# Pauses between gathers, a bias row in bf16 limbs, and a block that advances by two parts

## The chip, the cores and the metric

The kernel runs on one core of a Trainium2 chip. The metric is the device time of one execution, in microseconds (us); before the change it is 374.39 us in the median of three runs (374.32 to 375.45). TensorE (PE) multiplies matrices, VectorE (DVE) and ScalarE (ACT) work elementwise, GpSimd (POOL) here mainly issues indirect DMAs (gathers), and SyncE (SP) issues the plain ones. Each engine works through its own queue in order.

## What is computed

Two graph layers over one graph of N = 2708 nodes with 128 features. The adjacency matrix `adj` is dense in form but has few entries; it holds each node's own loop and is divided by its row sums.

```
# layer 0, hyperbolic
XW   = mobius_matvec(W, X)
sq   = sum(XW * XW, -1);  gamma = 2 / max(1 - sq, EPS)
nominator   = A_hat @ (gamma * XW)
denominator = _clamp_abs(A_hat @ (gamma - 1))
m    = mobius_scalar_mul(0.5, nominator / denominator)
AXW  = mobius_scalar_mul(A_hat.sum(-1), m)
x    = layernorm(x + expmap0(relu(logmap0(AXW))))
# layer 1, message passing
s, d = x @ msg_w[:, :D].T,  x @ msg_w[:, D:].T
messages   = gelu(s[:, None, :] + d[None, :, :] + msg_b)
aggregated = einsum('ijd,ij->id', messages, adj)
h    = gelu(concat([x, aggregated], -1) @ upd_w.T + upd_b) + x
x    = layernorm(x + (layernorm(h) * ln_w + ln_b))
```

The messages exist for all pairs of nodes, but only those with an entry in `adj` count.

## The kernel before, in words

The nodes lie in 22 row blocks of 128. **Layer 0** goes through the blocks one after the other. For each, SP's queue brings a block of the transposed matrix (1408 KB), TensorE multiplies it densely (`mp`, L339), and ScalarE turns it into signs (`sgn`, L334). From the signs TensorE and VectorE make keys (L366) and take from them the list of the block's entries, in tiles of 128 edges, 99 tiles in all. VectorE writes the places of the entries in memory (`F`, L464), and a gather per tile fetches their values from `adj` in DRAM into `V` (99 gathers, L197). The end of layer 0 (`layer0_end`, in three chunks of blocks) forms the first layer norm, the products s and d, and writes d into `table_dram`; the table's first ten blocks are there earlier than the rest.

**Layer 1** works through 26 messages of up to four tiles (512 edges). `fetch` issues the gathers of a message, one per tile, each of 128 rows of 512 bytes from `table_dram` into one of seven rooms `dd`. `messages` then takes one of them: X = R s per tile on TensorE (L687, R the one-hot matrix of receiving rows), the weighted one-hot matrix `rv` per tile on VectorE (L689), dd = X + dd on VectorE (L692), a Gelu over the whole room on ScalarE (L693), and a matmul per tile that adds up the rows of a block (`mp`, L702). After it come a `fetch` for a later message, and a `step`.

A block whose sums are complete becomes a generator, `node`, in `queue`. Its parts are a copy of the sums to SBUF (`agT`, L622), `update` (L566 to L570: two or three f32 matmuls, the bias row as a matmul of one partition, L569, and a Gelu), `first` (adding x, the statistics) and, with the last block of a group, `finish` (L576 to L606): the two layer norms of the group and the output DMA on SP's queue. The groups have 8, 6, 4, 2 and 2 blocks. `step` advances each queued generator by one part. `messages` also calls it when a fourth set of sums would be open.

The first nine messages use only early blocks of the table and the early tiles of the first eight blocks; their gathers are issued during layer 0, from block 14 on, and they themselves run while the last chunk of layer 0 ends. `whole` becomes non-empty when the table is complete; only then are the other messages fetched. The last six messages follow the count of entries that decides whether a dense path, not taken with these inputs, is needed. In the code's order the calls stand in one stream, but a scheduler orders the instructions of each engine by priority, as far as their data allow.

Every gather goes through one helper, `gather` (L195 to L202). After the indirect DMA it puts three writes of one f32 column on POOL's queue (L202), tied to the gather by `issue_after` and given a high priority, so that they follow it on the queue at once; they write to a tile `gap` that nothing reads. `ones`, a 128x128 f32 tile, is written by POOL at the start (L125); it serves the bias row, the count at the end, and `touch`, which calls a function once on ScalarE so that its table is loaded early.

Of the kernel before, what the change touches and what calls it, by code (L numbers as in the profile page):

```python
# [9 lines left out]

F32 = mybir.dt.float32
U32 = mybir.dt.uint32
BF16 = mybir.dt.bfloat16
I32 = mybir.dt.int32
AF = mybir.ActivationFunctionType
OP = mybir.AluOpType
AX = mybir.AxisListType

P = 128
# [16 lines left out]
SPLIT, BITS = 10, 16  # L36
# [42 lines left out]
def hyperbolic_then_message_kernel(  # L79
# [10 lines left out]
    nc = tc.nc  # L90
    N, D = adj.shape[0], P
    assert N % 2 == 0
    NB = (N + P - 1) // P
# [27 lines left out]
    ident = const.tile([P, P], F32, name="ident")  # L121
    make_identity(nc, ident)

    ones = const.tile([P, P], F32, name="ones")
    nc.gpsimd.memset(ones, 1.0)  # L125

    nhalf = const.tile([P, 1], F32, name="nhalf")
    nc.gpsimd.memset(nhalf, -0.5)
    ones_b = const.tile([P, P], BF16, name="ones_b")
    nc.gpsimd.memset(ones_b, 1.0)  # L130
    tri = const.tile([P, P], BF16, name="tri")
# [59 lines left out]
    of_block = {b: [l for l, v in enumerate(LISTS) if v[0] == b] for b in range(NB)}  # L191


    gap = [const.tile([P, 3], F32, name=f"gap{k}") for k in range(2)]

    def gather(o, src, at, kind):
        last = nc.gpsimd.indirect_dma_start(  # L197
            out=o, out_offset=None, in_=src, in_offset=bass.IndirectOffsetOnAxis(ap=at, axis=0)
        )
        with tc.issue_after(last.ins), tc.high_priority():  # L200
            for k in range(3):
                nc.gpsimd.memset(gap[kind][:, k : k + 1], 0.0)  # L202

    mx = big.tile([P, NB, D], F32, name="mx")
    y = big.tile([P, NB, D + 2], F32, name="y")
# [2 lines left out]
    def bank(name, bufs=2):  # L208
        return ps.tile([P, 512], F32, name=name, bufs=bufs)
# [11 lines left out]
    def cols(n):  # L221
        count[0] += 1
        return sc.tile([P, NB], F32, name=f"c{count[0]}")[:, :n]
# [46 lines left out]
    def touch(func, after):  # L270

        nc.scalar.activation(cols(1), after[:, 0:1], func)
# [4 lines left out]
    fin = ctx.enter_context(tc.tile_pool(name="fin", bufs=4))  # L277


    ss_x, ss_m = cols(NB), cols(NB)  # L280
    touch(AF.Ln, ones)
    quads = [(g, min(4, NB - g)) for g in range(0, NB, 4)]
    for g, n in quads:
        mp = bank("kx")
# [188 lines left out]
    def layer0_end(b0, b1):  # L473
# [2 lines left out]
        n = b1 - b0  # L476
        sb = slice(b0, b1)
        count[0] = 0
        touch(AF.Ln, ones)

# [80 lines left out]
    def update(h, k, b, ags):  # L563
        up = bank("sel", 1)
        s = slice(b * P, (b + 1) * P)
        nc.tensor.matmul(up[:, :D], lhsT=x1T[:, s], rhs=wT[:, 2, :], start=True, stop=False)  # L566
        for ag in ags:
            nc.tensor.matmul(up[:, :D], lhsT=ag, rhs=wT[:, 3, :], start=False, stop=False)
        nc.tensor.matmul(up[:, :D], lhsT=ones[0:1, :], rhs=rowvec["ub"][0:1, :], start=False, stop=True)  # L569
        nc.scalar.activation(h[:, k, :], up[:, :D], AF.Gelu)  # L570

    def finish(h, b0, n, pool, last):
# [57 lines left out]

    queue = []

    def step():

        for g in list(queue):
            if next(g, queue) is queue:
                queue.remove(g)

# [31 lines left out]
    def fetch():  # L670

        if len(rooms) < (len(work) if whole else ahead):
            dd = edge.tile([P, 4, P], F32, name="dd", bufs=RING)
            for k, (_, t, *_) in enumerate(work[len(rooms)]):
                gather(dd[:, k, :], table[: SPLIT * P] if t in soon else table, J[:, t : t + 1], 1)
            rooms.append(dd)

    def messages():

        q, ts = done[0], work[done[0]]  # L680
        done[0] += 1
        w = len(ts)
        dd = rooms[q][:, :w, :]
        X = bank("kx" if q >= ahead and q % 2 else "X").rearrange("p (t d) -> p t d", d=D)[:, :w, :]
        rv = edge.tile([P, 4, P], F32, name="rv", bufs=2)
        for k, (b, t, *_) in enumerate(ts):
            nc.tensor.matmul(X[:, k, :], lhsT=R[:, t, :], rhs=s_nm[:, b, :], start=True, stop=True)  # L687

            nc.vector.tensor_scalar(  # L689
                rv[:, k, :], iotaN, rid[:, t : t + 1], V[:, t : t + 1], op0=OP.is_equal, op1=OP.mult  # L690
            )
        nc.vector.tensor_tensor(dd, X, dd, op=OP.add)  # L692
        nc.scalar.activation(dd, dd, AF.Gelu)  # L693
        for k, (b, t, first, final, before) in enumerate(ts):
            mine = before or b >= EARLY
            if first:
                while len(sums) > 2:
                    step()
                sums[b] = bank("mp", 3)
                if mine:  # L700
                    own(b, sums[b])
            nc.tensor.matmul(  # L702
                sums[b][:, :P], lhsT=dd[:, k, :], rhs=rv[:, k, :], start=(first and not mine), stop=final
            )
            if final and before:
                nc.scalar.copy(gd[:, b, :D], sums.pop(b)[:, :P])
            elif final:
                g0, gn = group[b]
                queue.append(node(gd[:, g0 : g0 + gn, :D], b - g0, b, g0, gn, [gd[:, b, :D]] if b < EARLY else []))
        fetch()  # L710
        step()


    ends, found, placed = [], [], []
# [91 lines left out]
    cnt = sc.tile([P, 2], F32, name="cnt")  # L806
    nc.vector.tensor_reduce(cnt[:, 0:1], signs, axis=AX.X, op=OP.add)
    nc.vector.tensor_reduce(cnt[:, 1:2], deg.rearrange("p l k -> p (l k)"), axis=AX.X, op=OP.add)
    bp = bank("sel", 1)
    nc.tensor.matmul(bp[:, 0:2], lhsT=ones, rhs=flags, start=True, stop=True)  # L810
    nc.tensor.matmul(bp[:, 2:4], lhsT=ones, rhs=cnt, start=True, stop=True)
# [115 lines left out]
```

## Time and profile before

| what | before |
|---|---|
| median of 3 runs | 374.39 us (374.32 to 375.45) |
| profiled execution: its time, its span | 370.8 us, 369.1 us |
| mean granted clock of TensorE | 0.886 |
| busy: PE, PEld, DVE | 295.7, 272.9, 276.9 us |
| busy: ACT, POOL | 199.5, 239.0 us |
| start of the first gather after layer 0 | 257.64 us |
| end of the last gather | about 340.3 us |
| last dd add, end of VectorE's last instruction | 344.06, 364.37 us |

The profiled execution is one of its own, somewhat shorter than the median; 1.7 us of it lie outside the span. A line of the page's fifth part, or of an answer for one line, reads: line of the kernel, engine, operation, output and inputs, count | busy us in all, mean ns of one | idle us of the engine just before it, and what ended most of this idle time. A line of a table of windows gives the stretch, its length, the busy time of each engine with its count of instructions, TensorE's granted clock as a share of full speed, the share of DMA and its GB/s. A line of a timeline gives the start, the duration, the engine, the line, the operation, and in brackets the idle time ahead of it.

### The profile page before, as it was taken

To read this page: it belongs to the slowest core of one execution; us is meant where nothing else is said; L and a number is where in the kernel's file an instruction comes from. 1 tells how busy PE (TensorE), PEld (TensorE's weight loads), DVE (VectorE), ACT (ScalarE), POOL (GpSimd) and SP (SyncE) were. 2 spreads that over 40 slices of the span, in tenths; PEclk is the share of its full clock that TensorE was granted. 3 is DMA by queue.
4 is the path that set the end of the run, shared out by engine and by line. 5 is a ranking of instruction groups with operands and counts; after the bars stand their busy time and mean duration, and the time that the engine had idled before them with its cause. 6 is when DMAs were issued, how large, how long until landed. Compare 5 with 4: busy or idle time off the path is not lost.

```text
span 369.1 us, 8354 instructions
## 1 busy us (share of the span) xinstructions
PE 295.7 (80%) x2427; PEld 272.9 (74%) x2427; DVE 276.9 (75%) x1544; ACT 199.5 (54%) x537; POOL 239.0 (65%) x889
## 2 busy tenths in 40 slices
PE   2618998999999999999998897409858997996700
PEld 3507998999999898999998797409747886995600
DVE  0998898978768796877787878983725586477994
ACT  2791476767756885987659394424411232225340
POOL 7500087988898717078889878940888888888000
PEclk9955999999999999999999998957985699599755
DMA  8900455244564472556675210100122122122211
GB/s 305 386 2 2 168 173 196 102 166 163 205 227 179 160 241 105 183 191 214 205 265 203 96 50 1 31 14 28 48 54 56 51 52 52 52 56 50 63 59 38
DMA packets 16016, 45.16 MB, mean 122 GB/s; under 512 B 5402, under 2 KB 10926, under 8 KB 13150
## 3 DMA queue, kind: packets, MB, share of 16 engines
q1 hardware_dynamic: 9486, 37.43, 27.8%
q0 software_dynamic: 6336, 6.55, 7.4%
q10 hardware_dynamic: 144, 0.60, 0.5%
q8 instruction: 20, 0.33, 0.3%
q14 instruction: 30, 0.25, 0.2%
HBM read 41.74 MB, written 2.83 MB: 121 GB/s over the span
## 4 chain that ended last, share of the span: by engine, by line
PE 52%; DVE 13%; DMA 11%; POOL 11%; ACT 9%; issue 3%; POOLq 0%; DVEq 0%; ACTq 0%; SPq 0%
PE mp L339 22%; POOL dd L197 9%; DMA aT<-in_adj_t_dram 8%; PE kx L366 6%; PE sel L454 5%; PE mp L702 4%; ACT sgn L334 3%; PE X L540 3%; PE X L687 3%; DMA dd<-table_dram,J 2%; PE kx L287 2%; POOL gap L202 2%; ACT junk L294 2%; DMA xT<-in_x_t_dram 1%; PE kx L360 1%
## 5 line engine op out<-in xcount | busy, mean ns | idle before, releaser
L197 POOL DMA_INDIRECT V<-in_adj_dram,F x99 | 95.8, 968 | 69.1 <-DVE F L464 44.8
L339 PE MATMUL mp<-y,aT 128*128 128x130 f32 x968 | 126.8, 283 | 1.6 <-DMA aT<-in_adj_t_dram 1.6
L339 PEld LDWEIGHTS mp<-y,aT 128*128 128x128 f32 x968 | 117.3, 194 | 2.0 <-DMA aT<-in_adj_t_dram 2.0
L197 POOL DMA_INDIRECT dd<-table_dram,J x99 | 96.2, 971 | 27.4 <-PE X L687 13.4
L334 ACT ACTIVATE sgn<-aT 128x2816 bf16<-128x2816 f32 x22 | 56.0, 2547 | 7.3 <-DMA aT<-in_adj_t_dram 7.2
L702 PE MATMUL mp<-rv,dd 128*128 128x128 f32 x198 | 33.2, 320 | 14.0 <-ACT dd L693 12.3
L366 PEld LDWEIGHTS <-sgn 128*128 128x128 bf16 x484 | 28.6, 100 | 17.2 <-issue 9.0
L702 PEld LDWEIGHTS mp<-rv,dd 128*128 128x128 f32 x198 | 29.4, 226 | 15.9 <-ACT dd L693 13.9
L366 PE MATMUL kx<-kd,sgn 128*128 128x128 bf16 x484 | 33.3, 223 | 7.5 <-ACT sgn L334 7.5
L202 POOL MEMSET gap<- 128x1 f32 x594 | 36.3, 123 | 0.1
L689 DVE TENSOR_SCALAR rv<-iotaN,rid,V 128x128 f32<-128x128 f32 x99 | 30.9, 359 | 4.0 <-PE mp L702 4.0
L693 ACT ACTIVATE dd<-dd 128x512 f32<-128x512 f32 (+2 forms) x26 | 15.7, 607 | 30.6 <-DVE dd L692 30.6
L454 PE MATMUL sel<-z,R 128*128 128x41 f32 (+5 forms) x198 | 29.0, 277 | 3.6 <-DVE R L430 2.3
L454 PEld LDWEIGHTS sel<-z,R 128*128 128x128 f32 x198 | 25.8, 192 | 6.1 <-DVE R L430 3.7
L425 ACT ACTIVATE work<-iota,mid 128x256 f32<-128x256 f32 (+3 forms) x54 | 28.2, 569 | 3.5 <-DVE mid L418 3.3
L374 DVE MAX8 top<-kx 128x8 f32<-128x128 f32 (+3 forms) x133 | 24.8, 226 | 2.9 <-PE kx L366 2.7
L687 PE MATMUL X<-mx,R 128*128 128x128 f32 x132 | 22.3, 305 | 0.5 <-DVE dd L692 0.5
L687 PEld LDWEIGHTS X<-mx,R 128*128 128x128 f32 x132 | 18.6, 209 | 1.9 <-DVE dd L692 0.6
L692 DVE TENSOR_TENSOR dd<-X,dd 128x512 f32<-128x512 f32 (+1 forms) x17 | 11.3, 670 | 10.7 <-DMA dd<-table_dram,J 10.3
L457 DVE TENSOR_TENSOR work<-sel,place 128x120 f32<-128x120 f32 (+11 forms) x29 | 11.2, 387 | 9.6 <-PE sel L454 9.1
L378 ACT ACTIVATE junk_s<-kx 128x384 bf16<-128x384 f32 (+2 forms) x25 | 12.1, 483 | 9.6 <-DVE top L374 7.8
L622 ACT COPY agT<-mp 128x128 f32<-128x128 f32 x22 | 5.8, 262 | 18.6 <-PE mp L702 15.5
(200 smaller groups left out, 578.8 us busy)
## 6 DMA issues: line engine op xcount, KB each, us to landing
aT<-in_adj_t_dram SPq DMA_DIRECT2D x22, 1408.0 KB, 6.4
V<-in_adj_dram,F POOLq DMA_INDIRECT x99
dd<-table_dram,J POOLq DMA_INDIRECT x99
xT<-in_x_t_dram SPq DMA_DIRECT2D x2, 704.0 KB, 5.5
x_sb<-in_x_nm_dram SPq DMA_DIRECT2D x2, 704.0 KB, 9.3
table_dram<-dt SPq DMA_DIRECT2D x5, 256.0 KB, 2.5
out_dram<-nom SPq DMA_DIRECT2D x4, 256.0 KB, 3.2
pk<-in_pack_dram ACTq DMA_DIRECT2D x1, 587.5 KB
```

The source lines that it names most:

```text
L197: last = nc.gpsimd.indirect_dma_start(out=o, out_offset=None, in_=src, in_offset=bass.IndirectOffsetOnAxis(ap=at, axis=0))
L202: nc.gpsimd.memset(gap[kind][:, k : k + 1], 0.0)
L334: nc.scalar.activation(sgn, aT, AF.Sign, accum_out=signs[:, b : b + 1])
L339: p = nc.tensor.matmul(op[:, : D + 2], lhsT=aT[:, j, :], rhs=y[:, j, :], start=(j == 0), stop=(j == NB - 1))
L366: nc.tensor.matmul(kp[:, i * P : (i + 1) * P], lhsT=sgn[:, j, :], rhs=kd[:, q, :], start=False, stop=(i == len(groups) - 1 and j == j1 - 1),)
L374: nc.vector.max(top[:, c : c + 8], seg[:, s, :])
L425: nc.scalar.activation(r0, iota[:, k0 * P : k1 * P], AF.Abs, scale=2.0, bias=mid[:, k : k + 1])
L454: nc.tensor.matmul(sp[:, k, :], lhsT=R[:, t0 + k0 + k, :], rhs=z, start=True, stop=True)
L687: nc.tensor.matmul(X[:, k, :], lhsT=R[:, t, :], rhs=s_nm[:, b, :], start=True, stop=True)
L689: nc.vector.tensor_scalar(rv[:, k, :], iotaN, rid[:, t : t + 1], V[:, t : t + 1], op0=OP.is_equal, op1=OP.mult)
L693: nc.scalar.activation(dd, dd, AF.Gelu)
L702: nc.tensor.matmul(sums[b][:, :P], lhsT=dd[:, k, :], rhs=rv[:, k, :], start=(first and not mine), stop=final)
```

## The change

It has three parts.

First, the pause. `gap` becomes a tile of 360 bytes per partition, written in one instruction. It follows each gather of V (kind 0) and those table gathers that are issued before `whole` is set (kind 1); table gathers after that have kind 2 and no pause. In the built order 133 gathers have a pause, 99 of V and 34 of the table, and the last 65 of the table have none.

Second, the bias row. At the start VectorE splits it into three bf16 values that sum to it, in three rows of a tile `ub3`. Line L569 becomes one matmul of three bf16 rows of ones with these three rows. `ones` in f32 is no longer made at the start, but by VectorE in a work tile ahead of the count at the end; `touch` for the logarithm uses `iotaN`. A tile `nhalf`, which nothing used, is gone.

Third, the steps. `step` takes a number of generators, all by default; after each message's `step()` a `step(1)` advances the oldest queued block by one more part.

```diff
-    ones = const.tile([P, P], F32, name="ones")
-    nc.gpsimd.memset(ones, 1.0)
-
-    nhalf = const.tile([P, 1], F32, name="nhalf")
-    nc.gpsimd.memset(nhalf, -0.5)
...
-    gap = [const.tile([P, 3], F32, name=f"gap{k}") for k in range(2)]
+    gap = [const.tile([P, 360], U8, name=f"gap{k}") for k in range(2)]
...
-        with tc.issue_after(last.ins), tc.high_priority():
-            for k in range(3):
-                nc.gpsimd.memset(gap[kind][:, k : k + 1], 0.0)
+        if kind < 2:
+            with tc.issue_after(last.ins), tc.high_priority():
+                nc.gpsimd.memset(gap[kind], 0.0)
...
+    ub3 = const.tile([3, D], BF16, name="ub3")
+    limb = small.tile([P, 4 * P], BF16, name="junk_s", bufs=1)[0:3, :D]
+    rest_ub, hold = (small.tile([P, 4 * P], F32, name="work", bufs=3)[0:3, :D] for _ in range(2))
+    nc.vector.tensor_copy(rest_ub, rowvec["ub"][0:3, :])
+    for i in range(3):
+        nc.vector.tensor_copy(limb, rest_ub)
+        if i == 0:
+            nc.vector.tensor_scalar(hold, limb, ident[0:3, 0:1], None, op0=OP.mult)
+        else:
+            nc.vector.scalar_tensor_tensor(hold, limb, ident[0:3, i : i + 1], hold, op0=OP.mult, op1=OP.add)
+        if i < 2:
+            nc.vector.tensor_tensor(rest_ub, rest_ub, limb, op=OP.subtract)
+    nc.vector.tensor_copy(ub3, hold)
...
-    touch(AF.Ln, ones)
+    touch(AF.Ln, iotaN)
...
-        nc.tensor.matmul(up[:, :D], lhsT=ones[0:1, :], rhs=rowvec["ub"][0:1, :], start=False, stop=True)
+        nc.tensor.matmul(up[:, :D], lhsT=ones_b[0:3, :], rhs=ub3, start=False, stop=True)
...
-    def step():
-
-        for g in list(queue):
+    def step(n=NB):
+
+        for g in queue[:n]:
...
-                gather(dd[:, k, :], table[: SPLIT * P] if t in soon else table, J[:, t : t + 1], 1)
+                gather(dd[:, k, :], table[: SPLIT * P] if t in soon else table, J[:, t : t + 1], 1 + len(whole))
...
         fetch()
         step()
+        step(1)
...
+    ones = small.tile([P, 4 * P], F32, name="work", bufs=3)[:, :P]
+    nc.vector.memset(ones, 1.0)
     bp = bank("sel", 1)
     nc.tensor.matmul(bp[:, 0:2], lhsT=ones, rhs=flags, start=True, stop=True)
```

More of the change, by code (lines that the diff above doesn't have):

```diff
@@ L12 @@
 U32 = mybir.dt.uint32
+U8 = mybir.dt.uint8
 BF16 = mybir.dt.bfloat16
@@ L478, in layer0_end @@
         count[0] = 0
-        touch(AF.Ln, ones)
+        touch(AF.Ln, iotaN)
         den, r = nom[:, sb, D], nom[:, sb, D + 1]
```

## The prediction

> **What bounds the kernel now.** I read the page first, for its groups of instructions, and then the chain of waits from 255 us on, because the change has one part that acts only there.
>
> ```profile
> span 369.1 us, 8354 instructions
> PE 295.7 (80%) x2427; PEld 272.9 (74%) x2427; DVE 276.9 (75%) x1544; ACT 199.5 (54%) x537; POOL 239.0 (65%) x889
> ...
> L197 POOL DMA_INDIRECT V<-in_adj_dram,F x99 | 95.8, 968 | 69.1 <-DVE F L464 44.8
> ...
> L197 POOL DMA_INDIRECT dd<-table_dram,J x99 | 96.2, 971 | 27.4 <-PE X L687 13.4
> ...
> L202 POOL MEMSET gap<- 128x1 f32 x594 | 36.3, 123 | 0.1
> ```
>
> The averages say TensorE, and for layer 0 that is so: the windows give PE 94.67 us of the 97 between 43 and 140. POOL has 65%, but in the V row it waits 44.8 us for layer 0's lists (F), in few long stretches: 9.7 us ahead of 137, 11.4 ahead of 158, 13.3 ahead of 257.6. In layer 1 it is otherwise. The windows from the start of layer 1 (columns: length, then PE, PEld, DVE, ACT, POOL busy, TensorE's clock) and POOL's timeline inside one of them:
>
> ```profile
> 275.00:290.00 15.00, 13.04 (x52) 11.63 (x53) 7.42 (x26) 3.35 (x10) 13.18 (x49) 0.50 0.22 55
> 290.00:308.00 18.00, 18.00 (x131) 16.21 (x130) 14.03 (x54) 5.67 (x17) 15.95 (x57) 0.95 0.20 52
> 308.00:327.00 19.00, 16.77 (x94) 15.30 (x92) 10.87 (x50) 4.49 (x13) 16.76 (x61) 0.73 0.21 52
> ```
>
> ```profile
> 279.16 0.94 POOL L197 DMA_INDIRECT dd<-table_dram,J  x1 [0.15 <-issue]
> 280.09 0.18 POOL L202 MEMSET gap<- 128x1 f32 x3
> 280.42 0.94 POOL L197 DMA_INDIRECT dd<-table_dram,J  x1 [0.15 <-issue]
> 281.37 0.17 POOL L202 MEMSET gap<- 128x1 f32 x3
> ```
>
> One gather every 1.266 us: 0.944 for itself, 0.17 for three writes, 0.15 in which POOL waits for nothing that shows. The first gather after layer 0 starts at 257.64, the last ends at about 340.3: 65 gathers in 82.7 us, 1.272 each. The chain from 255 us to the end gives the gathers 29.0%, the pause 5.2% and "issue" 7.1%; VectorE's dd add waits for landing rows 7 times, 17.3 us, as the waits show:
>
> ```profile
> DVE dd L692 <- DMA dd<-table_dram,J: 17.3, 7, 4.2
> ```
>
> So layer 1 goes at the gathers' pace; then, from the last dd add (344.06) to VectorE's last instruction (364.37), 20.3 us of VectorE's chain (two layer norms); then the output DMA, to 369.1.
>
> **What the Trainium skill says.** "Perfetto Trace Analysis", section "DMA Instruction — SWDGE (GPSIMD)": the recorded end is when the last DSP has written its descriptors, and there is no start marker. So the 0.944 us may leave out part of a gather's work. This trace agrees: after an idle POOL, a gather's record starts 0.27 to 0.31 us after the write of F it waited for (45.80 to 46.11, 74.53 to 74.81). "SBUF — State Buffer", section "Who interferes with whom": the port pair shared by VectorE and GpSimd is an exclusive lock, which tensor_scalar can hold or wait for in its two-port mode. The trace shows little of it: the rv write (L689) takes about 405 ns instead of 334 if it starts about 0.5 to 0.65 us into a gather, else the same inside and outside of one. "VectorE: DVE Perf Modes", "Zero memsets can be issued as uint32": one cycle per element whatever the type. That is of VectorE, but POOL's rows agree: 128 elements take 201 ns in f32, 194 in bf16.
>
> **Part 1a, no pause in layer 1 (65 gathers).** In 185 of 198 cases the distance from a gather's end to the next start is 321 to 323 ns, also where the third write lasted until 472: it is not the writes' ends that count. The writes start 28 ns apart, 3 x 28 = 84 ns; the rest, 0.237, is about the lead seen after idle (0.27 to 0.31, some of it the semaphore's). I take it that the lead belongs to the gather and stays: 0.944 + 0.237 = 1.18 a gather. Bounds: 0.945 if the lead overlaps the gather before, 1.266 if it grows to what the pause was. Value: 64 x 0.086 = -5.5 us. Cover: TensorE. From 290 to 308 it is 18.00 of 18.00 busy, and can keep the new pace only because part 2 takes work out of it.
>
> **Part 1b, one write of 360 bytes in layer 0 (133 gathers).** The trace has no such write. From 128x1 (94 ns) to 128x128 (201) a write grows 0.84 ns per element; 360 byte elements occupy 28 + 302 = 0.33 us, the gap is 0.33 + 0.237 = 0.57, the period 1.51. If the bytes go four at a time, 90 elements: 0.10, gap 0.34, period 1.29. I take 1.51. It is hidden in the three idle stretches, 34.3 us together, so long as POOL has caught up by 257.6. Replaying the recorded gathers with their ready times: at a gap of 0.53 the last one is out of the way at 256.8, at 0.57 at 259.3 (1.6 late), at 0.65 at 264.6 (7.0 late), at 0.70 at 269.7 (12.1). In the changed order of the queue, in which V and table gathers mix differently, the same sum at 1.51 ends at 256.2. Between 0 and +1.6: I take +0.8. The first consumers (dd adds at 225.4 to 264.5) have slack: the gather that came at 210.7 would come at 227.6, still before its use.
>
> **Part 2, bias row.** Twice a 1x128 f32 pass for each of 22 updates:
>
> ```profile
> L569 PE MATMUL sel<-pk,ones x44: 270/372/578, 278.5 to 349.6; 1*128 1x128 f32 x44
> ```
>
> The pair advances the chain by 0.41 to 0.43 us (0.72 at half clock); one bf16 pass I estimate at 0.08, from the weight load of the bf16 row L366 (100 ns) with its matmul beside it. So -0.35 x 22 = -7 us of TensorE, nearly all beside gathers. On the end path lie one or two updates: -0.5 (0 to -1). The limbs cost some 11 VectorE operations on three rows at the start, in the waits of two root chains. But in the built order ScalarE loads one activation table more (nine, not eight) as its logarithm now touches iotaN, ready later: 1.283 us a load, on a path that runs through ScalarE from 13.5 to 25.7, of which 0.82 was idle. I take +0.5 (0 to +1.3). The ones that a late VectorE write makes again costs 0.2 us beside waits: nothing, or 0.2 were VectorE the bound there.
>
> **Part 3, two parts for the oldest block.** More instructions of finished blocks stand before each message's successor, fewer after the last. In the built order 119 VectorE instructions are left after the last dd add instead of about 144. By their durations (0.15 to 0.34 us) the 25 are worth 3.1 us, and 20.3 becomes 17.2. They must now fit before: VectorE has 63.2 us busy of the 86 between 257 and 343, so 66 of about 81, and that holds; but the last adds will be held up somewhat by norms ahead of them in VectorE's queue. Other queues: a block's update can now follow its copy (L622, 262 ns on ScalarE) within one message, with the next X matmuls queued behind on TensorE, who feed the next dd add; in the built order other matmuls mostly stand between. The norm's last part issues an output DMA on SP's queue, where by then nothing else is; POOL's queue isn't passed. For all of this +0.7 (0 to +2). With part 2: -3.1 - 0.5 + 0.7 = -2.9.
>
> **Sum**, against the profiled execution: -5.5 + 0.8 + 0.5 - 2.9 = -7.1 on a span of 369.1, so 362.0, and with the 1.7 us around it 363.7 instead of 370.8. The median of the runs is 374.39; the same difference gives 367.3.
>
> **Rivals.** *A, the lead overlaps.* POOL's queue is about two gathers ahead, which speaks for it; that the lead is there after a queued write too speaks against. At 0.98 us, 65 gathers would save 18.6, but TensorE has 72.5 us busy from 257 to 343 and keeps at least 65.5 without the bias passes, with half clock in places: 12 us at most, so 374.4 - 12 + 0.8 + 0.5 - 2.9 = 360.8. *B, the pause is not what sets the pace* (the lead grows, or TensorE, full from 290 to 308, takes its place): only the end's gain is left, 374.4 - 2.9 + 1.3 = 372.8; with a third of the pace 371. *C, slower: pauses in layer 0 that POOL cannot catch up.* The place is the stretch from 158 us to the first gather of layer 1. It decides from a gap of about 0.67 on: there layer 1 starts 8.5 us late and eats the gains. At 0.70 it is 12.1 - 8.0 = +4.1, so 378.5. For it: a byte write may cost more than the f32 slope says, and no row shows one longer than 1x1. Against: bf16 costs no more than f32. The same sign would come of a VectorE held up by unbroken gathers; the flat durations of L689 speak against it.
>
> **Chances.** Forecast 0.50 (364 to 370), A 0.20 (358 to 363), B 0.16 (370.5 to 374), C and its like 0.14 (375 to 382). A measurement of this kernel tells about 0.3% from no change, 373.3 to 375.5. The range reaches into A and to the upper edge of B, 359.5 to 373.5; beyond it I leave some 0.2. Faster 0.80, same 0.06 (B's edge), slower 0.14.
>
> **What will show it.** POOL's timeline after 258: starts 1.18 apart means the lead stays, 0.95 to 1.0 is A, 1.25 is B. In layer 0, a gap of 0.57 or 0.34, and the first gather of layer 1 at 257.6 plus the start's 0.5, or later, which is C. L569 with 22 passes. From the last dd add to VectorE's end 17 us. If the period falls and the end doesn't, the wait at dd L692 will have moved from DMA to TensorE. I am wrong if layer 1 starts more than 3 us late, or VectorE's rv rows grow beyond 0.45 us.

## The result, and the profile after

The changed kernel is slower: 376.68 us in the median of 20 runs (373.86 to 379.0) against 372.55 in 20 runs of the kernel before beside them (369.65 to 375.6). The ratio is 1.0124, with a 95% interval of 1.0097 to 1.0151, so about 4.6 us more. The profiled execution took 378.13 us, in a span of 376.3; that of before took 370.8. Runs of one kernel spread over some 5 us here, and one profile is one draw from that: differences of 2 or 3 us between two traces say nothing by themselves, and times are compared below by their ratios.

The page after, with the rows that answer to those of before (the gathers now stand at L194, the pause at L199, rv at L701):

```profile
span 376.3 us, 7851 instructions
PE 290.7 (77%) x2405; PEld 266.5 (71%) x2405; DVE 289.3 (77%) x1555; ACT 200.8 (53%) x538; POOL 259.2 (69%) x426
...
L194 POOL DMA_INDIRECT V<-in_adj_dram,F x99 | 95.3, 963 | 55.4 <-DVE F L476 39.5
...
L194 POOL DMA_INDIRECT dd<-table_dram,J x99 | 96.1, 971 | 29.0 <-issue 20.0
...
L199 POOL MEMSET gap<- 128x360 uint8 x133 | 56.9, 428 | 0.1
...
L701 DVE TENSOR_SCALAR rv<-iotaN,rid,V 128x128 f32<-128x128 f32 x99 | 33.9, 399 | 4.6 <-PE mp L714 3.4
```

The gathers cost what they did. The 133 pauses cost more than the 594 short writes, 56.9 us instead of 36.3. In front of the dd gathers "issue" has grown from 11.8 to 20.0 us: with no pause behind them, they wait for nothing that shows. VectorE is busy for 12 us more, and its rv row has a mean of 399 ns instead of 359. Before, that row was:

```profile
L689 DVE TENSOR_SCALAR rv<-iotaN,rid,V 128x128 f32<-128x128 f32 x99 | 30.9, 359 | 4.0 <-PE mp L702 4.0
```

POOL's timeline in layer 1 shows where the first part of the gain went (start, duration, and in brackets the idle time ahead):

```profile
282.66 0.95 POOL L194 DMA_INDIRECT dd<-table_dram,J  x1 [0.31 <-issue]
283.92 0.95 POOL L194 DMA_INDIRECT dd<-table_dram,J  x1 [0.30 <-issue]
285.17 0.95 POOL L194 DMA_INDIRECT dd<-table_dram,J  x1 [0.30 <-issue]
286.42 0.95 POOL L194 DMA_INDIRECT dd<-table_dram,J  x1 [0.30 <-issue]
```

A gather starts every 1.25 us, with 0.30 of unexplained idle time between two, where with the pause it was 1.27. The three short writes had cost 0.02 us, not 0.086: they lay in time that POOL spends anyway. The ten traces from chips of this pace agree: from the first gather of layer 1 to the last dd add it is 84.9 to 85.3 us in the six that have no pause there, and 86.2 to 86.9 in the four that have one.

And VectorE and POOL in layer 0, about 248 us, from two answers of the timeline of the same kernel:

```profile
247.94 0.95 POOL L194 DMA_INDIRECT V<-in_adj_dram,F  x1 [0.16 <-issue]
248.88 0.46 POOL L199 MEMSET gap<- 128x360 uint8 x1
249.50 0.95 POOL L194 DMA_INDIRECT V<-in_adj_dram,F  x1 [0.16 <-issue]
```

```profile
247.91 0.22 DVE L260 SCALAR_TENSOR_TENSOR c<-c,c 128x4 f32<-128x4 f32 x1
248.05 0.89 DVE L701 TENSOR_SCALAR rv<-iotaN,rid,V 128x128 f32<-128x128 f32 x1
248.31 0.63 DVE L260 SCALAR_TENSOR_TENSOR c<-c,c 128x4 f32<-128x4 f32 x1
248.38 0.63 DVE L701 TENSOR_SCALAR rv<-iotaN,rid,V 128x128 f32<-128x128 f32 x1
249.00 0.16 DVE L260 SCALAR_TENSOR_TENSOR c<-c,c 128x4 f32<-128x4 f32 x1
```

An rv write that takes 0.34 us alone starts at 248.05, 0.11 us into a gather, and lasts until 248.94: to 0.05 after the gather's end at 248.89. The small instruction behind it waits with it. I call this a hold. For comparison two rv writes of the kernel before, beside a gather that has three short writes behind it:

```profile
234.33 1.02 POOL L197 DMA_INDIRECT dd<-table_dram,J  x1
```

```profile
234.52 0.33 DVE L689 TENSOR_SCALAR rv<-iotaN,rid,V 128x128 f32<-128x128 f32 x1
234.86 0.54 DVE L689 TENSOR_SCALAR rv<-iotaN,rid,V 128x128 f32<-128x128 f32 x1
```

The one that starts 0.19 us into the gather takes its usual 0.33; the one that starts 0.53 into it lasts until just after the gather's end.

By stretches, from the two traces (blocks are counted from 0): block 2's signs, which the expectations below call block 1's, come at 46.0 us instead of 44.5, block 14's at 159.2 instead of 154.6, the last write of the table at 265.7 instead of 254.4, the first gather of layer 1 at 268.90 instead of 257.64. From there to the last dd add it is 85.1 us instead of 86.4, and from that add to VectorE's end 17.7 instead of 20.3. So layer 0 lost some 11 us in these two executions, layer 1 gained 1.3 and the end 2.6.

### The profile page after: what moved, and what is told of

Its sections match the earlier page's. It is cut to its first block, busy times and chain, and to the rows that moved or that the text cites. A ratio compares the mean times of both kernels' runs of the same rounds, so it can differ in the third digit from the quotient of the medians.

```text
span 376.3 us, 7851 instructions
## 1 busy us (share of the span) xinstructions
PE 290.7 (77%) x2405; PEld 266.5 (71%) x2405; DVE 289.3 (77%) x1555; ACT 200.8 (53%) x538; POOL 259.2 (69%) x426
## 5 line engine op out<-in xcount | busy, mean ns | idle before, releaser
L194 POOL DMA_INDIRECT V<-in_adj_dram,F x99 | 95.3, 963 | 55.4 <-DVE F L476 39.5
L351 PE MATMUL mp<-y,aT 128*128 128x130 f32 x968 | 129.0, 286 | 4.3 <-DMA aT<-in_adj_t_dram 4.3
L351 PEld LDWEIGHTS mp<-y,aT 128*128 128x128 f32 x968 | 119.0, 196 | 6.0 <-DMA aT<-in_adj_t_dram 4.6
L194 POOL DMA_INDIRECT dd<-table_dram,J x99 | 96.1, 971 | 29.0 <-issue 20.0
L199 POOL MEMSET gap<- 128x360 uint8 x133 | 56.9, 428 | 0.1
L714 PE MATMUL mp<-rv,dd 128*128 128x128 f32 x198 | 33.1, 317 | 18.8 <-ACT dd L705 17.2
L714 PEld LDWEIGHTS mp<-rv,dd 128*128 128x128 f32 x198 | 28.3, 218 | 21.4 <-ACT dd L705 19.2
L701 DVE TENSOR_SCALAR rv<-iotaN,rid,V 128x128 f32<-128x128 f32 x99 | 33.9, 399 | 4.6 <-PE mp L714 3.4
L466 PE MATMUL sel<-z,R 128*128 128x41 f32 (+5 forms) x198 | 29.7, 279 | 4.5 <-DVE R L442 4.0
L704 DVE TENSOR_TENSOR dd<-X,dd 128x512 f32<-128x512 f32 (+1 forms) x17 | 11.3, 671 | 12.8 <-DMA dd<-table_dram,J 7.1
L699 PE MATMUL X<-mx,R 128*128 128x128 f32 x132 | 20.6, 293 | 0.5 <-DVE dd L704 0.5
L699 PEld LDWEIGHTS X<-mx,R 128*128 128x128 f32 x132 | 17.6, 201 | 1.1 <-DVE dd L704 0.6
L442 DVE TENSOR_SCALAR R<-work,deg 128x512 f32<-128x512 f32 (+3 forms) x32 | 17.4, 557 | 0.8 <-ACT work L437 0.4
```

The costliest lines, as they stand in the source:

```text
L194: last = nc.gpsimd.indirect_dma_start(out=o, out_offset=None, in_=src, in_offset=bass.IndirectOffsetOnAxis(ap=at, axis=0))
L199: nc.gpsimd.memset(gap[kind], 0.0)
L351: p = nc.tensor.matmul(op[:, : D + 2], lhsT=aT[:, j, :], rhs=y[:, j, :], start=(j == 0), stop=(j == NB - 1))
L466: nc.tensor.matmul(sp[:, k, :], lhsT=R[:, t0 + k0 + k, :], rhs=z, start=True, stop=True)
L701: nc.vector.tensor_scalar(rv[:, k, :], iotaN, rid[:, t : t + 1], V[:, t : t + 1], op0=OP.is_equal, op1=OP.mult)
L714: nc.tensor.matmul(sums[b][:, :P], lhsT=dd[:, k, :], rhs=rv[:, k, :], start=(first and not mine), stop=final)
```

## Experiments: which part, and why

Two theories for layer 0 were put against each other, and a third beside them. **L (hold)**: the long write keeps VectorE's two-port instructions waiting. **Q (queue)**: the pause's length alone makes POOL late. **B**: the limbs at the start and the moved steps cost it (this is not the prediction's rival B). A first set took the change apart.

**Three columns again in layer 0**, all else as in the changed kernel:

```diff
-    gap = [const.tile([P, 360], U8, name=f"gap{k}") for k in range(2)]
+    gap = [const.tile([P, 3], F32, name=f"gap{k}") for k in range(2)]
...
-                nc.gpsimd.memset(gap[kind], 0.0)
+                for k in range(3):
+                    nc.gpsimd.memset(gap[kind][:, k : k + 1], 0.0)
```

> The changed kernel with the old pause in layer 0 (three f32 columns after each of the 133 paused gathers, in place of 360 bytes); the rest of the change stays. Theory L (lock): the write of 360 bytes keeps VectorE's two-port instructions waiting until the gather has ended, and layer 0 grows by that; then VectorE's rv rows before 257 us fall back from some 0.5 us to 0.36 on the mean, the last table write comes at 255 to 256 us and not at 265.7, and the time is 0.990 to 0.996 of before (pace of layer 1 -1.3 us, end -2.9, start +1). Theory Q (queue): POOL's longer period alone makes the gathers late; the same time here, but VectorE's rows stay as long as they are now. Theory B (start and order): the loss comes from the limbs at the start and the moved steps; then it stays at 1.01 of before.

Measured: 0.9904 of before (0.9867 to 0.9941), 369.76 us. B falls: with limbs and steps in place the kernel is faster than before. Setting the two ratios against each other (1.0124 / 0.9904), the 360 bytes cost 2.2%, some 8 us. The rv rows of VectorE between 20 and 257 us, first of the changed kernel, then of this one:

```profile
L701 DVE TENSOR_SCALAR rv<-iotaN,rid,V 128x128 f32<-128x128 f32 x24 | 11.0, 538 | 1.5 <-DMA V<-in_adj_dram,F 1.1 <-PE mp L714 0.4
```

```profile
L702 DVE TENSOR_SCALAR rv<-iotaN,rid,V 128x128 f32<-128x128 f32 x24 | 8.0, 355 | 0.0
```

The mean falls from 538 to 355 ns; in the kernel before it is 372:

```profile
L689 DVE TENSOR_SCALAR rv<-iotaN,rid,V 128x128 f32<-128x128 f32 x24 | 8.5, 372 | 0.0
```

So the hold goes with the 360 bytes, as L says; Q had these rows stay as long as they were. The last table write came at 258.9, later than I expected, but 6.8 us before that of the changed kernel.

**360 bytes in the kernel before**, up to the end of layer 0, with three columns afterwards, bias and steps untouched:

```diff
-    gap = [const.tile([P, 3], F32, name=f"gap{k}") for k in range(2)]
+    gap = [const.tile([P, 360], U8, name=f"gap{k}") for k in range(2)]
+    gap3 = const.tile([P, 3], F32, name="gapt")
...
-            for k in range(3):
-                nc.gpsimd.memset(gap[kind][:, k : k + 1], 0.0)
+            if kind < 2:
+                nc.gpsimd.memset(gap[kind], 0.0)
+            else:
+                for k in range(3):
+                    nc.gpsimd.memset(gap3[:, k : k + 1], 0.0)
...
-                gather(dd[:, k, :], table[: SPLIT * P] if t in soon else table, J[:, t : t + 1], 1)
+                gather(dd[:, k, :], table[: SPLIT * P] if t in soon else table, J[:, t : t + 1], 1 + len(whole))
```

> The kernel before with one change: 360 bytes in place of three columns after the gathers that are issued while the table is incomplete; the later ones keep the three columns, bias and steps are as before. L: VectorE's busy time before 257 us grows by 10 us or more, the last table write comes 7 to 10 us later than 254.4, time 1.02 to 1.03 of before. Q: VectorE's rows unchanged, the table write at 254 to 256, only the first gather of layer 1 is late, time 1.01. B: 1.00.

Measured: 1.0121 (1.0057 to 1.0185). The one edit makes the kernel slower by itself, by less than L's 1.02 to 1.03. The sum of VectorE's durations from 20 to 257 us grows by 19 us (instructions that stand together count twice in it: as busy time it is 195.3 us instead of 191.9), and the last table write comes at 263.4, where Q expected 254 to 256. The profile is that of the slowest of the six runs, 382.15 us against a median of 378.12, so its times support those of the changed kernel's trace and prove nothing alone.

**No pause in layer 1**, in the kernel before:

```diff
-        with tc.issue_after(last.ins), tc.high_priority():
-            for k in range(3):
-                nc.gpsimd.memset(gap[kind][:, k : k + 1], 0.0)
+        if kind < 2:
+            with tc.issue_after(last.ins), tc.high_priority():
+                for k in range(3):
+                    nc.gpsimd.memset(gap[kind][:, k : k + 1], 0.0)
...
-                gather(dd[:, k, :], table[: SPLIT * P] if t in soon else table, J[:, t : t + 1], 1)
+                gather(dd[:, k, :], table[: SPLIT * P] if t in soon else table, J[:, t : t + 1], 1 + len(whole))
```

> The kernel before with one change: no pause after the last 65 table gathers. All theories: a start every 1.25 us instead of 1.27, so 64 x 0.02 = 1.3 us less at most, ratio 0.9955 to 1.0. If VectorE's rv rows in layer 1 get longer than 0.36 us without the pause, unbroken gathers hold VectorE up, and the ratio is above 1.

Measured: 0.9939 (0.9908 to 0.9969). The gathers stand 1.25 us apart; from the first gather of layer 1 to the last dd add it is 85.1 us instead of 86.4. The interval's upper end, -1.2 us, fits this; the ratio is a little better. The rv rows after 257 us take 359 ns, so unbroken gathers do not hold VectorE more.

**The bias row alone**, in the kernel before (the limbs, one bf16 matmul at the bias row, `touch` on iotaN; the diff is that of the change without pauses and steps).

> The kernel before with the bias row as three bf16 limbs alone, with all that goes with it (the limbs at the start, touch on iotaN). L and Q: start 0.3 to 1.2 us later (one table load more on ScalarE, limb operations held up to 3 us on VectorE), TensorE relieved by 22 x 0.35, end -0.5: ratio 0.997 to 1.003. B: 1.005 or more, with block 1's signs (44.5 us before) 1.5 us later.

Measured: 0.9998 (0.9966 to 1.0031). Block 2's signs came 2.3 us later, at 46.8, and VectorE's chain at the end took 19.9 us instead of 20.3.

**The second step alone**, in the kernel before:

```diff
-    def step():
-
-        for g in list(queue):
+    def step(n=NB):
+
+        for g in queue[:n]:
...
         fetch()
         step()
+        step(1)
```

> The kernel before with one change: the oldest queued block moves by one more part after each message. From the last dd add to VectorE's end 17.7 us instead of 20.3, as in the changed kernel, layer 0 untouched: 0.991 to 0.996 of before. If the moved parts hold up the messages, the last dd add is later by more than 2 us and the ratio is near 1.

Measured: 0.9979 (0.9957 to 1.0001), so -0.8 us, where I expected more. From the last dd add to VectorE's end it is 20.55 us, no less than before, although only 120 of its instructions start after that add, where before it was 141. The waits of VectorE after 344 us say why:

```profile
DVE nom L616 <- ACT nom L570: 3.0, 2, 2.0
```

It waits 3.0 us for the last blocks' Gelu, which hangs on their updates on TensorE; before, this wait was 0.4. In the five traces from chips of this pace that have both the step and the one-pass bias row, the chain takes 17.67 to 17.83 us, and this wait is 0.2 to 0.4; in the five that lack one or both it takes 19.9 to 22.8. So the fewer instructions pay off only with the shorter update: parts 2 and 3 work together, each alone gives little. For each part alone this is one trace, and is no more than that.

Then the pause's length was parted from the hold.

**Twelve short writes**, about as long a pause in pieces:

```diff
-    gap = [const.tile([P, 360], U8, name=f"gap{k}") for k in range(2)]
+    gap = [const.tile([P, 12], F32, name=f"gap{k}") for k in range(2)]
...
-                nc.gpsimd.memset(gap[kind], 0.0)
+                for k in range(12):
+                    nc.gpsimd.memset(gap[kind][:, k : k + 1], 0.0)
```

> The changed kernel with twelve writes of one f32 column in place of the one of 360 bytes: by 28 ns a write the gap is 0.237 + 12 x 0.028 = 0.57 us, the same pause as the bytes give (0.578), in twelve short pieces. It parts length from hold. Theory L (the long write itself holds VectorE's two-port instructions): period 1.52 as now, but VectorE's rv rows before 257 us back at 0.36 to 0.42 us on the mean, the last table write at 257 to 261, the time 0.985 to 1.0 of before. Theory Q (the longer period makes the gathers late, and late V values and rows do the harm): as slow as the changed kernel, 1.01 to 1.02, with the rv rows at 0.36.

Measured: 1.0115 (1.0063 to 1.0167), as slow as the changed kernel. The gap is 0.577 us in most cases, as worked out, but 30 of the 132 gaps before layer 1 are longer, mostly about 0.77, so that their mean is 0.619, against 0.591 in the changed kernel. And the hold is gone:

```profile
L702 DVE TENSOR_SCALAR rv<-iotaN,rid,V 128x128 f32<-128x128 f32 x24 | 8.2, 367 | 1.8 <-DMA V<-in_adj_dram,F 1.0 <-PE mp L715 0.8
```

The mean is 367 ns, as before the change (372), and the last table write comes at 258.6. So L falls in the form in which I stated it: a pause of about this length makes the kernel as slow without the hold. That it would cost exactly as much at exactly the same length is not shown: over the 65 gathers after 158 us the longer mean is worth some 1.6 us, by my estimate from the two means there, 0.617 and 0.592. The trace shows gathers that are late. POOL from 257 us on:

```profile
258.78 0.95 POOL L194 DMA_INDIRECT dd<-table_dram,J  x1 [0.15 <-issue]
259.73 0.42 POOL L200 MEMSET gap<- 128x1 f32 x12
260.50 0.95 POOL L194 DMA_INDIRECT V<-in_adj_dram,F  x1 [0.34 <-DVE dd L705]
261.44 0.42 POOL L200 MEMSET gap<- 128x1 f32 x12
262.02 0.95 POOL L194 DMA_INDIRECT V<-in_adj_dram,F  x1 [0.15 <-issue]
262.97 0.57 POOL L200 MEMSET gap<- 128x1 f32 x12
263.90 0.95 POOL L194 DMA_INDIRECT dd<-table_dram,J  x1 [0.35 <-issue]
```

POOL comes straight from paused gathers into layer 1, whose first gather is that at 263.90: 5.3 us after the last table write, where before it was 3.2, after 13 us of idle POOL. A gather for V runs as late as 262.02; before the last was at 243.27. The lateness that one sees is 2 us, though, not 8. This profile is the quickest of its kernel's seven runs (373.3 against a median of 376.1) and the profile with three columns the slowest of its ten (371.8 against 369.8), which takes away most of the distance between them; where the rest of the usual loss lies is not seen.

**90 words in place of 360 bytes:**

```diff
-    gap = [const.tile([P, 360], U8, name=f"gap{k}") for k in range(2)]
+    gap = [const.tile([P, 90], F32, name=f"gap{k}") for k in range(2)]
```

> The changed kernel with one write of 90 f32 elements, the same 360 bytes in a quarter of the elements. By 0.84 ns an element the gap falls to about 0.34 us. Q: period as before, so no lateness, 0.990 of before. L: VectorE is held only as long as one write is short: if holding starts with the write's place in the queue and lasts to the gather's end, rv rows stay at about 0.5 us, the time near 1.005; if its length counts, rv rows 0.36 to 0.40 and 0.990 to 0.995.

Measured: 0.9938 (0.9912 to 0.9963). The same bytes in a quarter of the elements give a gap of 0.353 us, no loss, and rv rows without the hold:

```profile
L701 DVE TENSOR_SCALAR rv<-iotaN,rid,V 128x128 f32<-128x128 f32 x24 | 8.3, 365 | 0.8 <-PE mp L714 0.8
```

So it is the number of elements that sets how long the write takes, and neither the bytes nor that it is one write does the harm. Whether a long write of f32 elements would hold VectorE as the 360 byte elements do was not tried: length and type changed together.

**No pause at all:**

```diff
-        if kind < 2:
+        if kind < 0:
```

> The changed kernel with no pause anywhere. Gathers 1.25 us apart where they are queued, in layer 0 too. L and Q: no write is left to hold VectorE, no lateness; rv rows 0.36, time 0.985 to 0.995 of before. If unbroken gathers by themselves hold VectorE more than gathers with three short writes do, rv rows in layer 0 exceed 0.40 us and the time 1.0.

Measured: 0.9897 (0.9837 to 0.9956). The pauses can go in layer 0 too: rv rows have 350 ns there. This version, the one with three columns and the one with 90 words are quicker than both kernels, and their intervals overlap.

**The runs that decide less.** Ten runs were to place the loss further. All of them landed on three other chips, on which the kernel before too took about 500 us, and their traces show long idle times on all engines: from 20 us on, VectorE stands still for more than 1.5 us at a time for some 163 us in all with late limbs, where it is 33 us in the trace of before. What these engines wait for there, the traces don't show. The edits, in the changed kernel: nine or sixteen columns (as twelve above), the long write up to the 69th gather of V and three columns after it, or the reverse:

```diff
+    gap3 = [const.tile([P, 3], F32, name=f"gapc{k}") for k in range(2)]
+    values = [0]
...
+        early = kind == 0 and values[0] < 69
+        values[0] += kind == 0
...
-                nc.gpsimd.memset(gap[kind], 0.0)
+                if early:
+                    nc.gpsimd.memset(gap[kind], 0.0)
+                else:
+                    for k in range(3):
+                        nc.gpsimd.memset(gap3[kind][:, k : k + 1], 0.0)
```

and, on three columns, the limbs made later, by the same instructions put into a function:

```diff
-    touch(AF.Ln, iotaN)
+    touch(AF.Ln, ones_b)
...
+            if b == 14:
+                limbs()
```

> The changed kernel with nine writes of one f32 column as the pause of layer 0: gap 0.237 + 9 x 0.028 = 0.49 us, period 1.44, no long write. The replay of the recorded gathers has POOL just caught up at a gap of 0.50. Theory Q (only the length of the pause counts, through gathers that come late at the start of layer 1): no lateness, 0.990 to 0.995 of before, as with three columns. If the length harms in proportion from the start (late V values and rows hold up VectorE in layer 0): some two thirds of the way from three columns (0.990) to twelve (1.0115), so 1.004. L (the long write's hold): 0.990.

> The changed kernel with its 360 bytes only after the first 69 gathers of V (up to about 158 us, where POOL has idle time to catch up), and three columns after the other 64 paused gathers. L: VectorE's two-port rows are held there; block 14's signs at 158 to 159 us as in the changed kernel instead of 156 with three columns, layer 0 about 3 us longer, time 0.998 to 1.002 of before. Q: POOL catches up before 158, so no cost: 0.990.

> The changed kernel with three columns after the first 69 gathers of V and its 360 bytes after the other 64 paused gathers (158 us to the start of layer 1). Q: the whole loss, 1.010 to 1.013 of before. L: the larger part of it, since VectorE is the busier in that stretch, about 1.003 to 1.008. With the run before, the two losses should add up to that of the changed kernel if the causes are separate.

> The kernel with three columns in layer 0 (0.990 of before), with the limbs made at block 14 instead of at the start, and touch on a tile of ones in bf16 that is ready early. L and Q alike: no ninth table load, first signs as before (44.5 us in block 1 and not 46), so 1 to 1.5 us less than with the limbs at the start: 0.985 to 0.990. If the start's delay is hidden by the wait for the matrix, 0.990.

> As the run of this edit before (three columns after the first 69 gathers of V, 360 bytes after the other 64 paused gathers), on another chip. Theory Q (gathers late at the start of layer 1): the whole loss, 1.010 to 1.013 of before. L (hold by the long write): about 1.003 to 1.008, with rv rows before 257 us at 0.5 us.

> As the run of this edit before (360 bytes only after the first 69 gathers of V, three columns after the other 64), on another chip. Q: 0.990, since POOL catches up before 158 us. L: 0.996 to 1.002, block 14's signs at 158 to 159 us and not 156.

> As the run of this edit before (nine short writes, gap 0.49 us), on another chip. Q: just no lateness, 0.990 to 0.995. Harm in proportion to length: 1.004. L: 0.990.

> As the run of this edit before (three columns in layer 0, limbs made at block 14, touch on bf16 ones), on another chip. 0.985 to 0.990 if the start's delay counts, 0.990 if it is hidden. By the table that the trace then shows, signs of block 1 at 44.5 us.

> The changed kernel with its 360 bytes only after the first 69 gathers of V, three columns after the other 64 paused gathers: hold of VectorE up to 158 us without gathers that are late at the start of layer 1. Theory L: block 14's signs at 158 to 159 us (156 with three columns), table complete at 259 to 261, 0.996 to 1.002 of before. Q: 0.990, block 14 at 156. Counts only on a chip where the kernel before takes 370 to 376 us.

> The changed kernel with sixteen short writes as the pause of layer 0: gap 0.237 + 16 x 0.028 = 0.69 us, no long write: gathers late at the start of layer 1 without hold. By the replay layer 1 starts some 10 to 12 us later than with three columns. Theory Q: 1.02 to 1.03 of before, VectorE's rv rows at 0.36, POOL without idle time ahead of the first gather of layer 1. L, with length harmless: 0.990 to 1.0. Counts only on a chip where the kernel before takes 370 to 376 us.

Measured, as ratios to the kernel before on the same chip: nine columns 0.9744 and 0.9740, long write early 0.9486, 0.9486 and 0.9502, long write late 0.9486 and 0.9458, sixteen columns 0.8588 (0.854 to 0.8636), late limbs 1.0115 and 0.9977. The first figure of each version, but for the sixteen columns, is from one chip, and counts only three of the 25 runs of the kernel before there; in the medians of all runs late limbs take 499.2 us on that chip, against 500.5, so the 1.0115 is no evidence of a loss. No theory of mine says this. Every version with a pause longer than three columns in layer 0 was quicker there, by up to 14%, though not in the order of the length: nine columns after all 133 gathers lengthen the pauses by more (133 x 0.17 us) than the bytes after 69 or 64 of them (69 x 0.26), and gain less. These numbers say nothing of the chips on which the change was measured, and whether late limbs help there stays open.

What they do tell is local, for it is the length of single instructions. I counted the rv writes that start 0.1 to 0.6 us into a gather and asked whether they end only after it. Up to the first gather of layer 1, with the long write queued behind the gather, they do in 11 of 11 cases in the changed kernel, 8 of 8 with the bytes alone, 11 of 12 in the first stretch of the three with the write early, 10 of 10 in the second stretch of the two with the write late. With short writes or none behind it: 5 of 10 before, 2 of 8 with three columns, 2 of 10 with twelve, 2 of 10 with 90 words, 0 of 7 with sixteen, 4 of 11 with no pause, 5 of 11 in the second stretch of the three with the write early. Over all twenty traces the split is sharper by the place of the start:

| start of the rv write, from the gather's start | 360 bytes queued behind | short writes, 90 words or none behind |
|---|---|---|
| 0.1 to 0.4 us | 28 of 29 held | 0 of 77 held |
| 0.4 to 0.6 us | 12 of 12 | 38 of 47 |

A gather alone holds VectorE only late in its time. The long write, while it still waits behind the gather, makes it a hold from early on.

## Why the prediction was wrong, step by step

Predicted were 367.3 us, in a range of 359.5 to 373.5, and a faster kernel; measured were 376.68, and a slower one. Both signs that I had named for being wrong came: layer 1 starts 11.3 us late in the trace, and the rv rows of layer 0 grow to 538 ns.

**Part 1a, the pause of layer 1: wrong.** The step that failed is "I take it that the lead belongs to the gather and stays: 0.944 + 0.237 = 1.18 a gather". The gap without writes is 0.306, the period 1.25: 64 x 0.02 = 1.3 us instead of 5.5. I had read 0.237 from subtracting three starts of 28 ns, and thought that what shows as "issue" stays the same whatever the queue holds. It is the upper bound that held, nearly: the idle time grows to what the pause was. This is rival B's condition; its time of 372.8 was not seen, because part 1b came on top.

**Part 1b, the pause of layer 0: wrong, and it decides.** The usual size of the pause was right: 0.57 worked out, 0.578 measured. That it is "hidden in the three idle stretches, 34.3 us together, so long as POOL has caught up by 257.6" failed: I took +0.8 (0 to +1.6), and the runs show some 8 us.

Two things were missing. First, POOL does not catch up. From about 160 us on it goes from gather to gather almost without a break in both slow kernels, so its end is the start of this stretch plus 65 periods. I put in the usual gather and the usual pause, 1.51 us. The mean there is 1.58 in both kernels, because some gathers and some pauses are longer, and the stretch began at 162.7 us in the changed kernel and at 158.9 with twelve short writes, not at 158.1. From my 256.2 these two terms lead to about 265 in the changed kernel and, with 2 us in which POOL waited, to about 264 with twelve writes (estimates from the two traces); the last pause ends at 265.06 and 263.54. A queue that comes out of the replay at 256.2, with 257.6 as its limit, has no room for an error of 0.07 us in each of 65 periods, and I wrote down the steep row of 0.65 without giving it its weight. I also misread the idle time: of the 44.8 us that POOL waits for F, 29.7 lie ahead of its first gather. Of the three stretches only that ahead of 158 is a wait for F; the profile puts the 9.7 us down to another VectorE instruction (L241), and the 13.3 ahead of 257.6 are, by the times, the wait for the table.

Second, I named the lock that the Trainium skill, "SBUF — State Buffer", section "Who interferes with whom", describes, and judged it by the rv rows of before, with three short writes. That page's rule, that tensor_scalar in its two-port form and GpSimd take the shared pair in turn for a whole instruction, agrees with rv rows of 0.34 us that last 0.89 up to 0.05 us after a gather's end. No trace shows whether rv runs in that form, and the page does not speak of a write that is only queued. A row that has only short writes behind its gathers could not show what a long one does.

How the two share the loss is not settled. In the changed kernel's trace the hold shows. POOL's timeline there, and the row of the table's writes (their last start is what counts):

```profile
263.69 0.95 POOL L194 DMA_INDIRECT dd<-table_dram,J  x1 [0.17 <-issue]
...
268.90 0.95 POOL L194 DMA_INDIRECT dd<-table_dram,J  x1 [3.84 <-PE X L699]
```

```profile
L559 SPq DMA_DIRECT2D table_dram<-dt x6: 359/378/433, 148.5 to 265.7; - x6
```

The same row with twelve short writes:

```profile
L560 SPq DMA_DIRECT2D table_dram<-dt x6: 359/377/433, 144.6 to 258.6; - x6
```

In the changed kernel POOL is idle for 3.8 us ahead of the first gather of layer 1. This gather waits for the table: it starts 3.2 us after the last write, as in the eight other traces from such chips in which POOL is idle there (3.2 to 3.3). The table's last write comes at 265.7 (263.4 with the bytes alone, in the slowest of its runs) where the seven other traces of those chips and that of before have 253.7 to 258.9. With twelve short writes the table is on time and POOL is late. The start of layer 1 waits for whichever is later, so the two don't add up, and taking away only one leaves the other. That is an argument from single traces, in keeping with the times; a long hold without late gathers was tried only where it tells nothing of the time.

**Rival C** had the right side, and POOL is late at the place that it named, from 158 us to the start of layer 1. That all of the loss lies there is not shown: in the changed kernel block 14's signs, at 159.2 us, are already 2.8 us later than with three columns (156.4). Its turning point of a gap of 0.67 was too high twice over: the gain it had to eat was not 8 us but 4 (-1.3 and -2.6 at the end), and the replay made too little of the pause. Its chance of 0.14 was too small.

**Part 2: right in sum.** I said +0.5 at the start and -0.5 at the end, and alone it is 0.9998. The start is later by 0.3 to 2.3 us at block 2 in the six traces with the limbs, and in the changed kernel's a limb operation at 14.84 us takes 3.01 us while POOL does its set-up work. The row of the bias matmul in the changed kernel:

```profile
L581 PE MATMUL sel<-ub,ones_b x22: 224/225/283, 288.3 to 359.8; 3*128 3x128 bf16 x22
```

One pass of 225 ns, where two of 372 stood.

**Part 3: right in sum, wrong alone.** From 20.3 to 17.7 instead of 17.2, in the changed kernel. The step alone gives 0.8 us, because VectorE then waits for the last update. I had counted the instructions left and not asked what they wait for. For VectorE's busy time from 257 to 343 us I took 63.2 us; the trace of before has 54.6, so there was more room than I reckoned with.

Without part 1b the forecast's other parts come to -1.0%, the 0.9904 of the first run: -3.6 us, where the sum without 1b was -7.9, and the missing 4.3 are nearly all part 1a's (4.2).

## What to carry to other kernels

Before a pause or any small operation is taken out between two others, ask whether what shows as its cost is time that the next operation needs anyway: here a gap of 0.322 us fell to 0.306. Before one is made longer because its engine has idle time, look at where that idle time lies and what is queued behind it, and reckon with the mean of a period, not its usual value, where the queue has no room: here 1.58 us and not 1.51. And look at the other engine that may share a port: twelve short writes and one long one differ in what they do to VectorE, even where the pause is about as long.

## What was not expected of the hardware

- Back to back, gathers of 128 rows start every 1.25 us though each shows 0.944: 0.306 us between two belong to no instruction in the trace.
- A write of 360 byte elements on POOL takes 413 ns in the median and makes a gap of 0.578; 90 f32 elements, as many bytes, take 188 and make 0.353. Time goes by elements, not bytes, as the Trainium skill, "VectorE: DVE Perf Modes", section "Zero memsets can be issued as uint32", says of VectorE.
- A write of 360 byte elements on POOL that is queued behind a gather holds VectorE's rv write (a tensor_scalar) during the gather, before the write itself is recorded: 28 of 29 that started 0.1 to 0.4 us into one, against 0 of 77 with short writes, 90 words or none behind the gather.
- On three chips every kernel took 430 to 501 us in the median, and there the versions with longer pauses were quicker (0.859 with sixteen writes). The cause is open.
